# Layer 2 of a conv-attention network: one more piece of experts beside the gathers of a graph, layer norms at the end of an attention head

## The chip, the core and the metric

The kernel runs on one core of a Trainium2 chip. The core has a matrix engine (TensorE, PE in the profile, with weight loads shown apart as PEld), a vector engine (DVE), an activation engine (ACT), GpSimd (POOL) and a queue engine (SP) that issues most of the DMAs. The metric is the device time of one execution in microseconds, and of several executions the median.

## The reference, cut to what matters

A feature map `x` of shape (2, 256, 48, 48) goes through four layers: a selective-scan layer, a convolution-attention layer, and two layers of token mixing and token-wise experts. The change touches layer 2. Its 4608 tokens (2 x 2304, width 256) first go through a split attention, where one third of the positions are queries, one third keys and one third values, and the outputs of three heads stand behind one another; then through a layer norm, a graph attention whose four scores per token choose two of four experts, and the experts:

```python
t = t + _L2_attn_ref(_ln_t(t), ...)      # _ln_t: layer norm over 256 channels
t = t + _L2_ffn_ref(_ln_t(t), ...)

# attention, for each of 3 heads
e = x @ W.T + b;  q, k, v = jnp.split(e, 3, axis=1)      # split along positions
attn = softmax(q @ k.T * SCALE);  out_h = attn @ v

# experts
agg = segment-softmax aggregation of h[src] over all edges (and loops), by dst
scores = layernorm(agg + b_gat).reshape(M, HEADS, NUM_EXPERTS).mean(1)
topk_s, topk_i = top_k(scores, 2);  w = softmax(topk_s)
for ei in range(4):
    g = where(topk_i == ei, w, 0).sum(-1)
    hh = gelu(x @ W1[ei] + b1[ei])
    out = out + g * (hh @ W2[ei] + b2[ei])
```

There are 1,048,576 edges with indices drawn from 0 to 65,535. Indices beyond the 4608 tokens are clipped for the source (so most edges start at the last token), and edges to targets that don't exist are dropped.

## The kernel before, in words

Activations lie with the 256 channels on 128 partitions twice and the 4608 tokens along the free axis, in pieces of 384 columns: 12 pieces, 6 for each of the two batch images. `E.xres` is the running sum, `E.xn` its layer norm.

**Split attention (`layer2_attn`, L700 to L815).** For each image `b` and head `h` PE computes queries (L750), then for six blocks of 128 rows the logits (L764); DVE takes the row maximum, ACT the exponential (L773), DVE the reciprocal and the product (L778), PE transposes the block (L782), and DVE and ACT copy it to `pT`. Behind the blocks stand the sum over the values (L796) and the output projection (L806), added to `E.xres`. While image 1 is worked on, the pieces of image 0 are finished, so their layer norm for the experts is done there: L757 makes two generators per head, and L787 and L788 step one of them after each block. A generator (`normalize_piece`, which uses `layernorm`, L90 to L113) has three steps: DVE adds the two halves (L96); PE takes the mean (L99), DVE subtracts (L100) and ACT squares; PE takes the variance (L107), ACT takes the root, DVE the reciprocal (L110) and the product (L111). The PSUM pool for it has one buffer. The six pieces of image 1 are normalized at the beginning of `layer2_ffn`, in pairs in lock step.

**Experts and graph (`layer2_ffn`, `graph_scores`).** What an expert gives for a token doesn't need the graph; only its weight `g` does. So the pieces of 384 tokens fall into four sorts, set by L1322:
- `pieces(0, AHEAD)`, two pieces, run while the node part of the graph is worked on.
- `pieces(AHEAD, BESIDE)`, four pieces, run beside the gathers. POOL gathers rows of two tables for the last edges of each list (L1050 and L1054, 64 each, `add_edges`); meanwhile `count_last` counts, in 32 groups, how many of the clipped edges go to each target: DVE writes one-hot rows in bf16 (L946, L950), PE sums them (L952, 32 matmuls a group). `behind_gathers` takes the steps of the expert pieces between these groups in proportion, `n_beside` steps over 32 groups; a piece has 24 steps.
- `pieces(BESIDE, EARLY)`, two pieces, behind the graph's last edges (L1080, L1082, L1086), while the scores are worked out on DVE.
- the last `12 - EARLY`, four pieces, `later`, with the weights known.

For the early pieces the four experts' outputs are written to DRAM (`y_d`, L1375) and read back by `join` (L1410), which spreads the weights over the partitions on PE (L1402), multiplies on DVE (L1411) and adds on POOL (L1412). The last loop takes each late piece with `EARLY / n_late` joins, two at a time, and steps the layer norms of finished pieces between its matmuls.

One early piece has 4 experts, each of 8 matmuls with Gelu on ACT (L1354, L1358) and 8 for the second product (L1369) with the bias on ACT (L1373).

The order on each engine is not the program's: a scheduler reorders instructions of a block by its own estimates of durations. In the kernel before, the first four chunks of eight edges in `add_edges` have their L1063 to L1072 between count groups, though they are written behind `beside()`.

Of the kernel before, what the change touches and what calls it, by code (L numbers as in the profile page):

```python
# [33 lines left out]
NCH = L // W  # L34
# [417 lines left out]
def normalize_piece(E, wp, ps, c, eps=1e-5):  # L452

    cs = slice(c * W, (c + 1) * W)
    yield from layernorm(E, wp, ps, E.xres[:, :, cs], E.xn[:, :, cs], eps)
# [230 lines left out]
@with_exitstack  # L686
def layer2_attn(ctx, E):

    nc, tc, p = E.nc, E.tc, E.p
    NH, D = 3, 768
    S = L // NH
    DT, ST, HW2 = D // P, S // P, S // 2
    scale = C**-0.5
    big = ctx.enter_context(tc.tile_pool(name="l2big", bufs=1))
    xn = E.xn
    gm = big.tile([P, NH, 2, 2 * C], F32, name="gm")
    ub = big.tile([P, NH, 4], F32, name="ub")  # L700
    with (
        tc.tile_pool(name="l2wt", bufs=2) as wts,
        tc.tile_pool(name="l2wps", bufs=2, space=PSUM) as ps,
    ):
        for h in range(NH):

            w_eo = wts.tile([P, DT, 2 * C], F32, tag="w_eo", name="w_eo")
            nc.sync.dma_start(w_eo[:, :, 0:C], p["W_embed"][h].rearrange("(k p) m -> p k m", p=P))
            nc.sync.dma_start(w_eo[:, :, C:], p["W_outT"].rearrange("(k p) m -> p k m", p=P))
            for m in range(2):  # L710
                pg = ps.tile([P, 2 * C], F32, tag="pg", name="pg")
                for k in range(DT):
                    nc.tensor.matmul(
                        pg, lhsT=w_eo[:, k, m * P : (m + 1) * P], rhs=w_eo[:, k, :],
                        start=k == 0, stop=k == DT - 1,
                    )
                nc.vector.tensor_copy(gm[:, h, m, :], pg)
            pu = ps.tile([P, 4], F32, tag="pu", name="pu")
            for m in range(4):
                for k in range(DT):  # L720
                    nc.tensor.matmul(
                        pu[:, m : m + 1], lhsT=w_eo[:, k, m * P : (m + 1) * P],
                        rhs=E.v("b_embed", h * DT + k, 1), start=k == 0, stop=k == DT - 1,
                    )
            nc.vector.tensor_copy(ub[:, h, 0:2], pu[:, 0:2])
            nc.vector.tensor_tensor(ub[:, h, 2:4], pu[:, 2:4], E.v("b_out"), ALU.add)

    act = ctx.enter_context(tc.tile_pool(name="l2act", bufs=2))
    wp = ctx.enter_context(tc.tile_pool(name="l2w", bufs=2))
    ps = ctx.enter_context(tc.tile_pool(name="l2ps", bufs=3, space=PSUM))  # L730
    pss = ctx.enter_context(tc.tile_pool(name="l2pss", bufs=2, space=PSUM))
    psn = ctx.enter_context(tc.tile_pool(name="l2psn", bufs=1, space=PSUM))

    for b in range(NB):
        t0 = b * L
        xv = act.tile([P, ST, C], F32, tag="xv", name="xv", bufs=1)
        for t in range(ST):
            o = t0 + 2 * S + t * P
            tp = ps.tile([P, C], F32, tag="mm", name="tp")
            for k in range(2):  # L740
                nc.tensor.transpose(tp[:, k * P : (k + 1) * P], xn[:, k, o : o + P], E.ident)
            nc.vector.tensor_copy(xv[:, t, :], tp)
        for h in range(NH):
            qq = act.tile([P, 2, S], F32, tag="qq", name="qq")
            for m in range(2):
                for g in range(2):
                    gs = slice(g * HW2, (g + 1) * HW2)
                    pq = ps.tile([P, HW2], F32, tag="mm", name="pq")
                    for k in range(2):
                        nc.tensor.matmul(  # L750
                            pq, lhsT=gm[:, h, k, m * P : (m + 1) * P],
                            rhs=xn[:, k, t0 + g * HW2 : t0 + (g + 1) * HW2], start=k == 0, stop=k == 1,
                        )
                    nc.scalar.activation(qq[:, m, gs], pq, AF.Identity, bias=ub[:, h, m : m + 1])


            norms = [normalize_piece(E, wp, psn, (b - 1) * NCH + c) for c in range(2 * h, 2 * h + 2) if b]  # L757
            pT = act.tile([P, ST, S], F32, tag="pT", name="pT", bufs=1)
            for t in range(ST):
                sp = pss.tile([P, 2, 512], F32, tag="sp", name="sp")  # L760
                for g in range(2):
                    o = t0 + S + g * HW2
                    for k in range(2):
                        nc.tensor.matmul(  # L764
                            sp[:, g, :HW2], lhsT=qq[:, k, t * P : (t + 1) * P],
                            rhs=xn[:, k, o : o + HW2], start=k == 0, stop=k == 1,
                        )
                mx = wp.tile([P, 1], F32, tag="mx", name="mx")
                nc.vector.tensor_reduce(mx, sp[:, :, :HW2], AX.XY, ALU.max)
                nc.vector.tensor_scalar(mx, mx, -scale, None, ALU.mult)  # L770
                pr = wp.tile([P, S], F32, tag="pr", name="pr")
                sm = wp.tile([P, 1], F32, tag="sm", name="sm")
                nc.scalar.activation(  # L773
                    pr.rearrange("p (g w) -> p g w", g=2), sp[:, :, :HW2], AF.Exp,
                    bias=mx, scale=scale, accum_out=sm,
                )
                nc.vector.reciprocal(sm, sm)
                nc.vector.tensor_scalar(pr, pr, sm, None, ALU.mult)  # L778
                for n in range(0, ST, 3):
                    tp = ps.tile([P, 3, P], F32, tag="mm", name="tp")  # L780
                    for j in range(3):
                        nc.tensor.transpose(tp[:, j, :], pr[:, (n + j) * P : (n + j + 1) * P], E.ident)  # L782
                    if n:
                        nc.scalar.copy(pT[:, n : n + 3, t * P : (t + 1) * P], tp)
                    else:
                        nc.vector.tensor_copy(pT[:, n : n + 3, t * P : (t + 1) * P], tp)
                if norms:  # L787
                    next(norms[t // 3])  # L788

            ox = act.tile([P, 2, S], F32, tag="ox", name="ox")  # L790
            for m in range(2):
                for g in range(2):
                    gs = slice(g * HW2, (g + 1) * HW2)
                    po = ps.tile([P, HW2], F32, tag="mm", name="po")
                    for n in range(ST):
                        nc.tensor.matmul(  # L796
                            po, lhsT=xv[:, n, m * P : (m + 1) * P], rhs=pT[:, n, gs],
                            start=n == 0, stop=n == ST - 1,
                        )
                    nc.scalar.copy(ox[:, m, gs], po)  # L800
            for m in range(2):
                for g in range(2):
                    o = t0 + h * S + g * HW2
                    py = ps.tile([P, HW2], F32, tag="mm", name="py")
                    for k in range(2):
                        nc.tensor.matmul(  # L806
                            py, lhsT=gm[:, h, k, C + m * P : C + (m + 1) * P],
                            rhs=ox[:, k, g * HW2 : (g + 1) * HW2], start=k == 0, stop=k == 1,
                        )
                    y = wp.tile([P, HW2], F32, tag="y", name="y")  # L810
                    nc.vector.scalar_tensor_tensor(
                        y, py, ub[:, h, 2 + m : 3 + m], xn[:, m, o : o + HW2], ALU.add, ALU.add
                    )
                    xr = E.xres[:, m, o : o + HW2]
                    nc.gpsimd.tensor_tensor(xr, xr, y, ALU.add)  # L815

# [496 lines left out]
def layer2_ffn(ctx, E, edges):  # L1315
# [3 lines left out]

    nc, tc, p = E.nc, E.tc, E.p  # L1320
    NX, FT = 4, 4
    AHEAD, BESIDE, EARLY = 2, 6, 8  # L1322
    big = ctx.enter_context(tc.tile_pool(name="l2fbig", bufs=1))
    xn = E.xn
    w1 = big.tile([P, NX, 2, 512], F32, name="w1")
# [12 lines left out]
    wp = ctx.enter_context(tc.tile_pool(name="l2fw", bufs=2))  # L1338
# [50 lines left out]
    psn = ctx.enter_context(tc.tile_pool(name="l2fpn", bufs=2, space=PSUM))  # L1389
# [50 lines left out]
    for i in range(n_late):  # L1440
# [5 lines left out]
        norms = chain.from_iterable(normalize_piece(E, late, psn, c) for c in done)  # L1446
# [498 lines left out]
```

## Time and profile before

| | us |
|---|---|
| three timed executions | 5452.36, 5459.55, 5462.36 (median 5459.55) |
| the profiled execution | 5504.47, span 5502.7, mean granted TensorE clock 0.949 |
| split attention of layer 2 | 3182 to 3515 |
| first two expert pieces, node part | 3515 to 3640 |
| gathers, count, four pieces | 3640 to 3933 |
| the edges' sums (L1086) | 3933 to 4010 |
| two pieces and the scores | 4010 to 4100 |
| joins and late pieces | 4100 to 4362 |

The stage limits are from the trace; layers 0 and 1 lie ahead of them and layer 3 behind. A row of the timeline gives start and duration in us, the engine, the line, the operation, output and inputs with shape, and how many instructions; in brackets stands how long the engine idled before and what released it. [...]

### The profile page before, as it was taken

The numbers are of one execution on the slowest core, as the hardware profiler recorded it, in microseconds if no ns is written. First come the engines' busy times: TensorE is split into PE (matmuls) and PEld (weight loads), VectorE is DVE, ScalarE is ACT, GpSimd is POOL, SyncE is SP. The second block draws the span as 40 slices with busy tenths as digits, with TensorE's granted clock in tenths as the row PEclk, the third lists the DMA queues.
The fourth block names the chain that finished last, engine by engine and source line by source line (L and its number), as shares of the span: only waits on it lengthen the run. The fifth ranks groups of instructions, "written<-read, shape, count | busy, mean of one in ns | idle before, by whom it ended". The sixth has DMA issues, their size and how long they took to land. (4 is left out here: it accounts for less than half of the span.)

```text
span 5502.7 us, 47222 instructions
## 1 busy us (share of the span) xinstructions
PE 4797.7 (87%) x15246; PEld 2649.9 (48%) x15246; DVE 3499.6 (64%) x5380; ACT 2371.5 (43%) x4935; POOL 2398.4 (44%) x1295
## 2 busy tenths in 40 slices
PE   7888788888877787879999999998799999998996
PEld 3444344444333343435555555565455555554664
DVE  4899988888999888999994234456534401212333
ACT  5767777666767566622222123322023322222220
POOL 3888887888989888830000000048412100001112
PEclk8999999999999899999999899999899999999997
DMA  4444444443444444421100100111111100001323
GB/s 155 166 171 177 165 178 160 160 157 137 173 150 173 150 161 153 151 100 37 41 26 2 39 1 0 37 38 24 14 58 46 46 6 6 9 6 23 83 76 80
DMA packets 173646, 486.56 MB, mean 88 GB/s; under 512 B 31487, under 2 KB 96516, under 8 KB 173124
## 3 DMA queue, kind: packets, MB, share of 16 engines
q1 hardware_dynamic: 165252, 471.82, 24.3%
q0 software_dynamic: 8128, 11.55, 1.6%
q8 instruction: 124, 2.03, 0.1%
q14 instruction: 142, 1.16, 0.1%
HBM read 416.44 MB, written 66.86 MB: 88 GB/s over the span
## 5 line engine op out<-in xcount | busy, mean ns | idle before, releaser
L344 PE MATMUL yp<-hc,ident 128*128 128x384 f32 x3072 | 1199.9, 523 | 293.7 <-DVE hc L390 253.8
L359 POOL TENSOR_TENSOR db<-dtu,bb 128x1536 f32<-128x1536 f32 x384 | 1333.3, 3473 | 45.5 <-issue 16.5
L344 PEld LDWEIGHTS yp<-hc,ident 128*128 128x128 f32 x3072 | 574.7, 198 | 875.3 <-DVE hc L390 451.3
L390 POOL TENSOR_TENSOR hc<-ho,cc 128x384 f32<-128x384 f32 x576 | 582.6, 1020 | 183.6 <-DVE ho L382 81.9
L390 DVE TENSOR_TENSOR hc<-hs,cc 128x384 f32<-128x384 f32 x960 | 501.3, 544 | 38.9 <-PE yp L344 37.7
L376 ACT ACTIVATE hs<-dt,negab 128x384 f32<-128x384 f32 x768 | 435.2, 582 | 92.6 <-DVE ho L385 41.4
L376 ACT ACTIVATE hs<-dt,negaf 128x384 f32<-128x384 f32 x768 | 434.6, 582 | 58.4 <-DVE hc L390 27.7
L385 DVE TENSOR_TENSOR_SCAN hs<-hs,state,db 128x384 f32<-128x384 f32 x400 | 396.6, 1015 | 55.8 <-POOL db L359 30.3
L382 DVE TENSOR_TENSOR_SCAN hs<-hs,state,db 128x384 f32<-128x384 f32 x400 | 397.1, 1014 | 30.0 <-POOL db L359 23.2
L1770 POOL DMA_INDIRECT xe<-xt_d,token x48 | 52.4, 1091 | 726.4 <-issue 715.0
L266 PE MATMUL mm<-xw,w_cv 128*128 128x384 f32 x768 | 288.8, 512 | 64.5 <-ACT xs L270 26.6
L1704 PE MATMUL po<-at,xtok 128*128 128x384 f32 x864 | 329.7, 506 | 7.7 <-ACT at L1702 7.5
L912 POOL PARTITION_ALL_REDUCE most<-most x1 | 0.4, 382 | 738.8 <-DVE most L911 738.8
L1354 PE MATMUL ph<-xn,w 128*128 128x384 f32 x768 | 292.9, 523 | 28.0 <-issue 10.4
L1695 PE MATMUL sp<-qT,xn 128*128 128x384 f32 x864 | 317.2, 486 | 0.0
L1702 ACT ACTIVATE at<-sp 128x384 f32<-128x384 f32 x216 | 104.9, 491 | 472.5 <-PE sp L1695 472.4
L1358 ACT ACTIVATE hid<-ph,vec 128x384 f32<-128x384 f32 x192 | 110.8, 582 | 338.8 <-PE ph L1354 254.5
L627 PE MATMUL pf<-t,wfc 128*128 128x384 f32 x768 | 255.4, 489 | 0.0
L646 PE MATMUL po<-hid,wfc 128*128 128x384 f32 x768 | 253.6, 486 | 0.0
L385 DVE TENSOR_TENSOR_SCAN ho<-hs,state,db 128x384 f32<-128x384 f32 x240 | 241.2, 1005 | 15.3 <-ACT hs L376 15.1
L382 DVE TENSOR_TENSOR_SCAN ho<-hs,state,db 128x384 f32<-128x384 f32 x240 | 240.3, 1001 | 6.3 <-ACT hs L376 6.2
L266 PEld LDWEIGHTS mm<-xw,w_cv 128*128 128x128 f32 x768 | 146.0, 196 | 192.7 <-ACT xs L270 43.2
(434 smaller groups left out, 7962.9 us busy)
## 6 DMA issues: line engine op xcount, KB each, us to landing
bb<-bcd SPq DMA_DIRECT2D x192, 768.0 KB
cc<-bcd SPq DMA_DIRECT2D x192, 768.0 KB
xw<-xi_d SPq DMA_DIRECT2D x24, 774.0 KB
w<-in_m_w SPq DMA_DIRECT2D x16, 1024.0 KB
y_d<-y SPq DMA_DIRECT2D x32, 384.0 KB
ye<-y_d SPq DMA_DIRECT2D x32, 384.0 KB
xi_d<-xz SPq DMA_DIRECT2D x48, 192.0 KB
z_d<-xz SPq DMA_DIRECT2D x48, 192.0 KB
```

What stands on the lines that cost most here:

```text
L266: nc.tensor.matmul(px, lhsT=w_cv[b, s][:, d * 4 + k, :], rhs=xw[:, d, o : o + W], start=k == 0, stop=k == 3,)
L344: nc.tensor.matmul(yp[d], lhsT=E.ident, rhs=hc, start=False, stop=summed[d] == NS)
L359: nc.gpsimd.tensor_tensor(db, bc(dtu[:, d, :], [P, GN, W], 1), bb, ALU.mult)
L376: nc.scalar.activation(hs, dt[:, d, :], AF.Exp, scale=nega[s][:, d * NS + n : d * NS + n + 1])
L382: nc.vector.tensor_tensor_scan(to, hs, db[:, j], init, ALU.mult, ALU.add)
L385: nc.vector.tensor_tensor_scan(to[:, ::-1], hs[:, ::-1], db[:, j, ::-1], init, ALU.mult, ALU.add)
L390: (nc.gpsimd if on_pool else nc.vector).tensor_tensor(hc, to, cc[:, j, :], ALU.mult)
L627: nc.tensor.matmul(pf, lhsT=wfc1[:, k, f * P : (f + 1) * P], rhs=t1[:, k, :], start=k == 0, stop=k == 1,)
L646: nc.tensor.matmul(po[m], lhsT=wfc2[:, f, m * P : (m + 1) * P], rhs=hid[:, i, :], start=f == 0, stop=f == 15,)
L1354: nc.tensor.matmul(ph, lhsT=w1[:, e, k, f * P : (f + 1) * P], rhs=xn[:, k, c * W : (c + 1) * W], start=k == 0, stop=k == 1,)
L1695: nc.tensor.matmul(sp, lhsT=xn[:, k, t0 + i * P : t0 + (i + 1) * P], rhs=qT[:, k, c * W : (c + 1) * W], start=k == 0, stop=k == 1,)
L1704: nc.tensor.matmul(po[m], lhsT=xtok[:, i, m * P : (m + 1) * P], rhs=at, start=i == 0, stop=i == MT - 1,)
```

## The change

The layer norms of image 0 no longer take a step after each block of a head of image 1. The two pieces of a head are normalized together, in lock step, at the head's end. And `EARLY` goes from 8 to 9 and `BESIDE` from 6 to 7: five pieces instead of four beside the gathers (120 steps instead of 96 over the 32 count groups), two behind the graph as before, and three late pieces with three joins each instead of four with two.

```diff
--- before.py
+++ after.py
@@ layer2_attn
-            norms = [normalize_piece(E, wp, psn, (b - 1) * NCH + c) for c in range(2 * h, 2 * h + 2) if b]
             pT = act.tile([P, ST, S], F32, tag="pT", name="pT", bufs=1)
             for t in range(ST):
...
                     else:
                         nc.vector.tensor_copy(pT[:, n : n + 3, t * P : (t + 1) * P], tp)
-                if norms:
-                    next(norms[t // 3])
...
                     xr = E.xres[:, m, o : o + HW2]
                     nc.gpsimd.tensor_tensor(xr, xr, y, ALU.add)
+
+            if b:
+                norms = [normalize_piece(E, wp, psn, (b - 1) * NCH + 2 * h + i) for i in range(2)]
+                for _ in zip(*norms):
+                    pass
@@ layer2_ffn
     NX, FT = 4, 4
-    AHEAD, BESIDE, EARLY = 2, 6, 8
+    AHEAD, BESIDE, EARLY = 2, 7, 9
```

## The prediction

> **What bounds the kernel now.** I read the page's busy shares first, then a table of windows over the stages that the change touches, then the waits of PE and DVE in the gather stage, then the rows themselves. PE is busy for most of the span:
>
> ```profile
> PE 4797.7 (87%) x15246; PEld 2649.9 (48%) x15246; DVE 3499.6 (64%) x5380; ACT 2371.5 (43%) x4935; POOL 2398.4 (44%) x1295
> ```
>
> The windows are split attention (3182 to 3515), gathers with count and four pieces (3640 to 3933), and joins with late pieces (4100 to 4362). Columns: length, then busy time and instructions of PE, PEld, DVE, ACT, POOL, then granted clock, DMA share, GB/s.
>
> ```profile
> 3182.00:3515.00 333.00, 303.94 (x1037) 181.91 (x1037) 132.61 (x255) 102.84 (x181) 23.86 (x24) 0.94 0.01 2
> ...
> 3640.00:3933.00 293.00, 242.06 (x1529) 162.53 (x1528) 173.42 (x105) 61.27 (x102) 235.29 (x128) 0.91 0.12 24
> ...
> 4100.00:4362.00 262.00, 253.65 (x706) 129.41 (x704) 125.20 (x124) 80.64 (x109) 61.60 (x35) 0.92 0.15 44
> ```
>
> The late stage is full on PE (254 of 262 us): whatever PE no longer does there is gained. The gather stage has 51 us of PE idle, so an extra piece may or may not fit in. Where that idle time lies (PE's waits, 3640 to 4000: total, times, longest):
>
> ```profile
> PE po L1369 <- ACT hid L1358: 29.4, 1, 29.4
> PE ph L1354 <- issue: 10.4, 6, 5.7
> PE ph L1354 <- ACT hid L1358: 5.5, 5, 3.5
> ```
>
> and the rows at the one long wait:
>
> ```profile
> 3920.01 0.95 POOL L1054 DMA_INDIRECT gd<-t_dst,didx  x1 [0.30 <-issue]
> 3926.26 0.20 DVE L957 COPY cnt<-cp 128x36 f32<-128x36 f32 x1 [44.22 <-remote]
> 3926.32 0.58 ACT L1358 ACTIVATE hid<-ph,vec 128x384 f32<-128x384 f32 x1 [34.71 <-remote]
> 3926.95 3.57 PE L1369 MATMUL po<-hid,w 128*128 128x384 f32 x5 [29.37 <-ACT hid L1358]
> ```
>
> The count's matmuls had ended at 3892.4, yet DVE's copy of the count and ACT's Gelu, which need nothing but PE's results, start at 3926.3, 5 us after the last gather. So PE's signals came late while POOL gathered without a pause (3883 to 3921). Whether timed executions lose these 29 us too is the main open question: many semaphore records are missing there, and the profiled execution took 5504.47 us, 44.9 us (0.8%) more than the median of 5459.55, which is what would follow if this wait and the smaller "issue" waits were the recorder's. Everything below is a difference, laid on the median. 0.2%, 10.9 us, is about what a measurement of this kernel can tell from no change.
>
> What paces POOL and DVE in that stage:
>
> ```profile
> 3837.07 0.94 POOL L1054 DMA_INDIRECT gd<-t_dst,didx  x1 [0.30 <-issue]
> 3838.32 0.95 POOL L1050 DMA_INDIRECT gs<-t_src,sidx  x1 [0.30 <-issue]
> 3840.82 4.52 POOL L1050 DMA_INDIRECT gs<-t_src,sidx  x1 [0.30 <-issue]
> ```
>
> ```profile
> 3779.84 0.19 DVE L1068 TENSOR_TENSOR e<-gs,gd 128x32 f32<-128x32 f32 x1 [9.86 <-DMA gd<-t_dst,didx]
> 3780.34 4.41 DVE L946 TENSOR_TENSOR ol<-lo,lo_ids 128x4096 bf16<-128x4096 bf16 x1
> 3806.96 0.19 DVE L1068 TENSOR_TENSOR e<-gs,gd 128x32 f32<-128x32 f32 x1 [16.23 <-DMA gd<-t_dst,didx]
> ```
>
> A gather with its gap takes 1.25 us alone and about 4.7 us beside DVE's one-hot L946 (4.42 us): each count group costs POOL some 3.45 us. The scheduler hoists the first four chunks' L1068 between count groups on DVE; each waits there for its chunk's sixteenth gather, with the next L946 queued behind it and PE's next count group behind that.
>
> **The late stage: four late pieces become three, with three joins each for two.** The rounds start on PE (L1395) at 4161.50, 4224.39, 4288.76; the steady period is 64.37 us. A late piece's own 70 matmuls take 45.2 us at 0.645 (two records of a matmul; eight matmuls took 5.16). A third join adds 4 spreads and 3 transposes, 3.1 us, and a further norm, 1.3: at least 4.4. Half the period's remainder, (64.37 - 45.2)/2 = 9.6, is the upper bound. I take 6.4, since joins run partly at the cold clock (L1402 rows of 0.91 for two records). Three rounds of 70.8 against four of 64.4: -45 us, bounds -51 and -36. The added POOL adds (4 x 1.81) and DVE multiplies (4 x 0.95) lie beside PE; at three joins POOL is busy 22 of 71 us. Without that cover the upper bound applies. The added DMAs, four y_d writes and four ye reads on SP's queue, move 3 MB at a DMA share of 0.12 to 0.15 with four ye buffers: nothing, or some 3 us if the first ye of a join is late.
>
> **The gather stage: a fifth piece.** It brings 64 matmuls x 0.645 = 41.3 us of PE; 16 Gelus and 8 bias adds on ACT (0.58 each, 14 us, ACT is 79% idle). PE gets 10 expert matmuls a group for 8, so a group's period is 2.02 + 6.45 = 8.5 us. The order of the built kernels also changes: before, the chunk waits on DVE stand around groups 16, 20 and 23; after, chunks 0 and 1 stand between groups 9 and 10, and chunks 2 and 3 both ahead of group 13. I walk POOL and DVE with the prices above from 3671.7, up to where nothing differs:
> - Chunk 1 needs gather 32. DVE stands idle from about 3704, POOL runs at 1.25 us, gather 32 ends at 3721, L946 number 10 ends at 3727.4; PE has run out of work some 18 us before.
> - L946 11 and 12 follow by 3741.4; by then 38 gathers are done. Chunk 3 needs number 64: 26 more at 1.25 end at 3774.8, L1068 1.4 us later as in the rows, L946 13 from 3776.8; group 13 on PE at 3782 after another 22 to 26 us of idling.
> - The last 20 groups: 20 x 2.02 + 202 x 0.645 = 170.7, to 3952.7; 2.7 us at the cold clock after the stall (8 records of L1354 took 5.49 us for 2.81) and hiccups of about 10 as now (15.55 us per two groups for 14.4): 3965, bounds 3950 and 3975.
> - Gathers 65 to 128 at 4.5 per 9.1 us end near 3908, before the count, so no unbroken run of gathers stands behind it.
>
> Today the stage ends at 3932.6, or at 3902.6 without the long wait. So it costs +33 us if timed runs have the wait, +63 if not; bounds of the walk +48 to +73 for the latter. The add_edges run behind it (77 us, DVE at 70) is unchanged and starts from the count's end either way. I take +63, for the 44.9 us reason above.
>
> A rule against a row: the Trainium skill, "SBUF — State Buffer", section "Who interferes with whom", says that a tensor_tensor with both inputs in SBUF blocks only GpSimd's reads, and infers that descriptor generation, which needs the write port, is not blocked by it. By that rule 128 gathers would take 160 us, no chunk would be waited for, and the extra piece would cost its 41 us, the sum then -8. The rows here disagree: L946 is a tensor_tensor and the gather beside it takes 4.52 us instead of 0.95, so the sum goes by the rows.
>
> **Split attention: norms at a head's end.** The same 12 pieces (b-1) are normalized; ACT, PE and DVE instructions are only moved. A head without norms has a pitch of 49.1 us (L806 at 3234.72 and 3283.83), those with them 54.1, 57.75, 54.5 and 55.4. Part of that is the tail's wait:
>
> ```profile
> 3267.67 0.84 PE L782 MATMUL tp<-ident,pr 128*128 128x128 f32 x6 [2.48 <-DVE pr L778]
> 3319.56 1.51 PE L782 MATMUL tp<-ident,pr 128*128 128x128 f32 x6 [4.25 <-DVE pr L778]
> 3377.04 1.51 PE L782 MATMUL tp<-ident,pr 128*128 128x128 f32 x6 [4.25 <-DVE pr L778]
> ```
>
> L110's 2.54 us reciprocal stands ahead of the last softmax block on DVE. In the order after, two such tails lose it (1.7 us each); a pair of norms moves instead to the next head's start, where Sqrt and Exp swap tables (1.28 us). Bounds -8 (four tails cleared at 1.8, less a little) and +3 (two swaps unhidden); I take -4, two tails. The PSUM pool of one buffer makes the second norm of a pair wait for the first: DVE's L100 and L111, with the next head's L778 queued behind. That is what would eat the gain. The last pair, behind the loop, stays.
>
> **Sum:** -45 + 63 - 4 = +14: 5459.55 + 14 = 5473.5 us. Its own range, with the bounds of each step partly cancelling: 5460 to 5490.
>
> **Rivals.**
> - A, faster: timed runs do have the 29 us wait, and it goes, since the gathers end before the count. -45 + 33 - 4 = -16: 5443.5. It decides as soon as more than 14 us of that wait is real. For it: PE issues single matmuls 1.2 to 1.4 us apart in bursts of gathers, in step with them. Against: the missing records and the slow profiled run.
> - B, much slower: if PE's signals truly stick behind an unbroken run of gathers, the new 26-gather wait may not end with gather 64: L946 13 misses its buffer's release until number 128. 64 x 1.25 = 80 us more: -16 + 80 = +64, 5523. Against: group 11, whose buffer it needs, ends while L946 12 still slows POOL.
> - C, no change: timed gathers are free of recording and take 0.95, not 1.25 (the 0.30 gap "issue"). The 48 gathers of the two waits shorten by 14 us: +14 - 14 = 0, 5459.5.
>
> **How the numbers follow.** Forecast 50%, A 25%, C 13%, B 12%. Of the forecast's 50, 34 are over +10.9 us, 15 within, 1 below; of A's 25, 21 below and 4 within; C 3 below, 6 within, 4 above; B all above. Faster 0.25, same 0.25, slower 0.50. The range 5436 to 5503 takes in A to 7 us below its value and the forecast with 13 us more than its own upper bound; B and a little of A's low end stay out.
>
> **What would show it.** Right: late rounds 70 to 72 us apart; DVE rows L1068 with waits of about 18 and 34 us; add_edges' matmuls starting near 3965; no wait near 29 us at the last gather; the tails' 4.25 us waits down to 2.5 in two heads. Wrong: rounds of 74 or more, chunk waits under 10 us, a DVE wait of 80 us, or a long wait that stays in the profile.

## The result, and the profile after

The changed kernel took 5465.55 us in the median of 20 runs (5456.7 to 5479.59), the kernel before 5457.02 beside it (5449.6 to 5468.12): a ratio of 1.0016, 95% interval 1.0009 to 1.0024, so 8.5 us slower, with an interval of 5 to 13. The forecast was 5473.5, +14.

The profiled executions say the opposite: 5470.04 us after, 5504.47 before. First the busy shares from the page of the changed kernel, then a table of windows over its three stages (columns as in the prediction):

```profile
span 5468.3 us, 47253 instructions
...
PE 4787.9 (88%) x15242; PEld 2647.6 (48%) x15242; DVE 3499.1 (64%) x5378; ACT 2368.7 (43%) x4941; POOL 2390.3 (44%) x1299
```

```profile
3176.00:3499.00 323.00, 298.30 (x1037) 178.60 (x1036) 134.04 (x255) 99.93 (x179) 23.79 (x24) 0.97 0.01 3
3623.00:3934.00 311.00, 274.83 (x1656) 185.35 (x1655) 173.06 (x104) 74.44 (x126) 225.46 (x128) 0.94 0.13 28
4101.00:4325.00 224.00, 216.50 (x574) 106.76 (x571) 123.51 (x121) 71.46 (x93) 67.92 (x39) 0.89 0.21 58
```

The late stage is 38 us shorter (262 to 224) and still full on PE. The gather stage now holds 275 us of PE work instead of 242. From the first gather to the edges' sums it takes 304.1 us (3629.53 to 3933.66) against 285.6 (3646.95 to 3932.58). Lines moved by one behind the attention: L947 is L946 of before, L1069 is L1068, L1396 is L1395.

The 29 us wait at the last gather is gone; PE's waits in the gather stage (total, times, longest) are now those for DVE:

```profile
PE cp L953 <- DVE oh L951: 33.6, 2, 21.2
PE po L1370 <- ACT hid L1359: 2.4, 1, 2.4
```

DVE's chunk waits stand behind them, in rows of the timeline, with PE's first matmul of group 13 below:

```profile
3683.57 0.19 DVE L1069 TENSOR_TENSOR e<-gs,gd 128x32 f32<-128x32 f32 x1 [5.39 <-DMA gd<-t_dst,didx]
3703.64 0.19 DVE L1069 TENSOR_TENSOR e<-gs,gd 128x32 f32<-128x32 f32 x1 [18.52 <-DMA gd<-t_dst,didx]
3734.43 0.19 DVE L1069 TENSOR_TENSOR e<-gs,gd 128x32 f32<-128x32 f32 x1 [11.45 <-DMA gd<-t_dst,didx]
3754.61 0.24 DVE L1069 TENSOR_TENSOR e<-gs,gd 128x32 f32<-128x32 f32 x1 [20.00 <-DMA gd<-t_dst,didx]
...
3760.37 2.19 PE L953 MATMUL cp<-oh,ol 128*128 128x36 bf16 x32 [21.16 <-DVE oh L951]
```

This is the walk of the prediction: 18.5 us for chunk 1, 11.45 + 20.0 for chunks 2 and 3 together, and PE idling 12.5 and 21.2 us behind them. The rounds of the late stage, and the first transpose of layer 3 behind them:

```profile
4101.22 0.49 PE L1396 MATMUL tp<-ident,g 128*4 128x128 f32 x3
...
4175.23 0.49 PE L1396 MATMUL tp<-ident,g 128*4 128x128 f32 x3
...
4245.54 0.49 PE L1396 MATMUL tp<-ident,g 128*4 128x128 f32 x3
...
4325.28 0.66 PE L1678 MATMUL tp<-ident,xn 128*128 128x128 f32 x4 [0.65 <-DVE xres L1436]
```

74.0, 70.3 and 79.7 us. Before, four rounds took 61.6, 62.9, 64.4 and 73.2 us, between these rows:

```profile
4099.92 0.49 PE L1395 MATMUL tp<-ident,g 128*4 128x128 f32 x3
...
4361.99 0.66 PE L1677 MATMUL tp<-ident,xn 128*128 128x128 f32 x4 [0.65 <-DVE xres L1435]
```

In the attention before, four tails waited 4.25 us or more. The prediction shows the first two; the other two are

```profile
3431.41 1.51 PE L782 MATMUL tp<-ident,pr 128*128 128x128 f32 x6 [4.26 <-DVE pr L778]
3487.60 1.51 PE L782 MATMUL tp<-ident,pr 128*128 128x128 f32 x6 [4.60 <-DVE pr L778]
```

After, the four are

```profile
3311.68 1.51 PE L780 MATMUL tp<-ident,pr 128*128 128x128 f32 x6 [1.84 <-DVE pr L776]
3368.97 1.37 PE L780 MATMUL tp<-ident,pr 128*128 128x128 f32 x6 [4.32 <-DVE pr L776]
3421.83 0.84 PE L780 MATMUL tp<-ident,pr 128*128 128x128 f32 x6 [1.79 <-DVE pr L776]
3472.91 0.84 PE L780 MATMUL tp<-ident,pr 128*128 128x128 f32 x6 [2.48 <-DVE pr L776]
```

so three of the four long waits went, 6.9 us together, and the stage from the first transpose (L741) to the last head's projection shrank from 323.0 to 312.6 us.

What is left to explain is why a trace that is 34 us shorter belongs to a kernel that is 8.5 us slower.

### The profile page after: what moved, and what is told of

It reads as the page before. It is cut to its first block, busy times and chain, and to the rows that moved or that the text cites. A ratio compares the mean times of both kernels' runs of the same rounds, so it can differ in the third digit from the quotient of the medians.

```text
span 5468.3 us, 47253 instructions
## 1 busy us (share of the span) xinstructions
PE 4787.9 (88%) x15242; PEld 2647.6 (48%) x15242; DVE 3499.1 (64%) x5378; ACT 2368.7 (43%) x4941; POOL 2390.3 (44%) x1299
## 5 line engine op out<-in xcount | busy, mean ns | idle before, releaser
L392 ACT COPY state<-hs 128x1 f32<-128x1 f32 x800 | 117.4, 155 | 277.3 <-DVE hc L390 275.5
```

## The experiments

Theory 1, as predicted: the 29.4 us wait is made by the recorder, and timed runs of the kernel before don't have it. Theory 2: it is in timed runs too. The chips decided between them in a way that neither had foreseen: **the kernel before takes about 5451 to 5457 us in the timed runs of some chips and 5501 to 5503 in those of others**. Recorded runs go with the timed ones: the kernel with 32 idle gathers more took 5449.55 us recorded beside a median of 5451.76 on a chip of the first kind, 5542.85 beside 5532.98 on one of the second. I call them prompt and late chips. Of the four jobs below, each on another chip, the first ran on a prompt one and the other three on late ones. Each chip was seen in one job only, so it is not shown that the chip, and nothing else in the job, makes the difference.

The comparison of the result ran on a prompt chip, by its 5457 us (which chip is not on record). The page of before that the prediction read is of the late kind. Besides its 5504.47 us and its wait, its list of DMAs lacks the time from issue to landing. So do the pages of all eight late runs, while the changed kernel's first page and those of the four prompt runs have it (before, then the changed kernel):

```profile
bb<-bcd SPq DMA_DIRECT2D x192, 768.0 KB
bb<-bcd SPq DMA_DIRECT2D x192, 768.0 KB, 4.2
```

| run | change against the kernel before | before there, us | ratio, 95% interval |
|---|---|---|---|
| e1_norms_only | attention part alone | 5450.93, prompt | 0.9988 (0.9979 to 0.9997) |
| e2_pieces_only | pieces alone | 5450.93, prompt | 1.0042 (1.0028 to 1.0055) |
| e3_more_gathers | 32 idle gathers more | 5450.93, prompt | 1.0002 (0.9993 to 1.0011) |
| e5_before_held | chunks held behind the count | 5450.93, prompt | 1.0008 (0.9999 to 1.0017) |
| e4_after_held | whole change, chunks held | 5502.20, late | 0.9921 (0.9905 to 0.9937) |
| e6_norms_held | attention part, chunks held | 5502.20, late | 0.9975 (0.9965 to 0.9984) |
| e7_piece_behind | ninth early piece behind the graph | 5502.20, late | 0.9994 (0.9985 to 1.0002) |
| e8_change | the whole change | 5501.04, late | 0.9999 (0.9987 to 1.0011) |
| e9_after_held_again | as e4_after_held | 5501.04, late | 0.9925 (0.9909 to 0.9941) |
| e10_more_gathers_again | as e3_more_gathers | 5501.04, late | 1.0058 (1.0043 to 1.0072) |
| e11_after_held_third | as e4_after_held | 5503.05, late | 0.9907 (0.9892 to 0.9922) |
| e12_norms_only_again | as e1_norms_only | 5503.05, late | 0.9978 (0.9968 to 0.9988) |

### Is the wait at the last gather real?

The edit, in `add_edges` of the kernel before:

```diff
     if beside is not None:
+        idle = ip.tile([P, 32, F], F32, name="idle")
+        for j in range(32):
+            nc.gpsimd.indirect_dma_start(
+                out=idle[:, j, :], out_offset=None, in_=t_src[:, :],
+                in_offset=bass.IndirectOffsetOnAxis(ap=sidx[:, j : j + 1], axis=0),
+            )
         beside()
```

> The kernel before, with 32 further gathers behind the 128 real ones, whose rows nobody reads; the order on PE, DVE and ACT is the same. They lengthen POOL's unbroken run behind the count by 32 x 1.25 = 40 us, to about 3961. Theory 1 (the 29.4 us wait of PE and DVE at the end of the run exists only while a profile is recorded): the profiled execution shows the wait grown to about 69 us, and the timed runs stay at those of before within 3 us, ratio 1.000. Theory 2 (the wait is there in timed runs too): both grow, timed runs by about 40 us, ratio 1.007.

The time stayed (1.0002). But the recorded execution did not do what theory 1 says: POOL gathers until 3955, and no long wait stands behind the count. DVE's copy of the count comes at once, and PE's waits from 3640 to the end of the edges' sums are 5.8 us at most (rows of the timeline):

```profile
3864.26 0.20 DVE L957 COPY cnt<-cp 128x36 f32<-128x36 f32 x1 [9.39 <-PE cp L952]
...
3954.35 0.94 POOL L1062 DMA_INDIRECT idle<-t_src,sidx  x1 [0.30 <-issue]
...
3960.05 7.07 PE L1360 MATMUL ph<-xn,w 128*128 128x384 f32 x12 [9.79 <-issue]
```

The 9.8 us in the last row stand behind the edges' sums. SP, ACT, DVE and PE all go on there within 0.7 us (3959.35 to 3960.05), some 4 to 5 us after the last idle gather. At the same place PE stands 5.5 us in the run of the attention part alone, on this chip and without idle gathers. So the idle gathers may cost some 4 us there, but not the 40 that theory 2 expects, and the recorder doesn't make the wait at the count. The same kernel was run on a late chip:

> The kernel before with 32 further gathers. If this is a chip on which the kernel before takes about 5502 us, and PE's signals there wait for POOL's unbroken run to end, the wait grows with the run: +40 us, ratio 1.007, in timed and profiled runs alike. If the wait there is of a fixed length, or if the chip is of the other kind: within 3 us, ratio 1.000.

There it costs 0.58%, 32 us, in timed runs (the expected 1.007 lies in the interval), and the wait has grown to 56.9 us (rows of the timeline):

```profile
3937.41 0.20 DVE L957 COPY cnt<-cp 128x36 f32<-128x36 f32 x1 [60.79 <-remote]
3948.61 0.58 ACT L1364 ACTIVATE hid<-ph,vec 128x384 f32<-128x384 f32 x1 [62.52 <-remote]
3949.25 6.07 PE L1375 MATMUL po<-hid,w 128*128 128x384 f32 x10 [56.90 <-issue]
...
3954.84 0.94 POOL L1062 DMA_INDIRECT idle<-t_src,sidx  x1 [0.30 <-issue]
```

On a late chip, then, DVE and ACT do go on late after PE's results while POOL gathers without a pause, and a longer run makes a longer wait. It grew by 27 us for 40 us of gathers; PE went on 6.5 us before the last one ended, so it isn't simply released by the end. The profile calls the releaser "remote"; whether the signal is sent late or taken late is not in the records.

One kernel, the attention part alone, was recorded on both kinds of chip. On the prompt one DVE's copy of the count waits for PE as in the row above, on the late one PE stands 33.3 us at the last gather (row of the first, then PE's wait in the second):

```profile
3863.55 0.20 DVE L958 COPY cnt<-cp 128x36 f32<-128x36 f32 x1 [9.39 <-PE cp L953]
```

```profile
PE po L1370 <- ACT hid L1359: 33.3, 1, 33.3
```

Why chips differ is open: no run looks at that.

### The two parts apart

The attention part alone is the change without its new `AHEAD, BESIDE, EARLY`:

> The attention part of the change alone (norms at a head's end; pieces as before). Theory: the two traces show the split attention 10.4 us shorter (PE's L741 to the last head's projection, 323.0 against 312.6), of which about 1.7 lies in a head without norms and is the granted clock; so the part by itself is worth 8 to 9 us: ratio near 0.9985, 5449 us against 5457. Rival: the shorter stage is the clock of one profiled execution, and the timed runs show nothing: ratio 1.000, within 2 us.

> The attention part alone. Theory: worth the same on either kind of chip, since its stage has no gathers: ratio 0.998 to 0.999. Rival (a gain of that size is the difference of two chips or clocks): 1.000.

It gains 0.12% on the prompt chip and 0.22% on a late one: 6.5 and 12 us, intervals 2 to 11 and 7 to 18. The stage is 312.3 and 312.6 us in these two traces, and 321.1 to 323.0 wherever the old order ran (the runs with 32 idle gathers, with the pieces alone, with four pieces held, and the kernel before). The rival (the difference of two chips or clocks, ratio 1.000) lies outside both intervals; the sizes agree with the 9 to 10 us of the traces within them.

The pieces alone are the kernel before with this one line changed:

```diff
-    AHEAD, BESIDE, EARLY = 2, 6, 8
+    AHEAD, BESIDE, EARLY = 2, 7, 9
```

> The fifth piece beside the gathers alone (norms as before). Theory: it costs what the whole change costs plus what the norms gain: 8.5 + 8.5 = +17 us, ratio 1.003. In its profile the gather stage lasts as long as after the change (304 us from first gather to the edges' sums), the late stage 224 instead of 262, and no PE wait of 20 us or more stands at the last gather. Rival (norms worth nothing): +8.5 us, ratio 1.0016.

1.0042 is +23 us (15 to 30). Two other traces of this job have the pieces as before: the run with idle gathers and the attention part alone. Against them the stretch from the first gather to the first join takes 470.3 us instead of 412.4 and 409.7, +58 and +61; the late stage takes 228.4 instead of 262.3 and 268.3, -34 and -40. The sums are +24 and +21. No PE wait of 20 us stands at the last gather, but two for DVE stand ahead of groups 10 and 13, as after the whole change. The expected +17 lies in the interval, the rival's +8.5 outside it.

### The same change on a late chip

> The changed kernel itself beside the kernel before on one chip. So far the chips are of two kinds: on one the kernel before takes 5451 us and no wait follows the last gather, on the other 5502 us with a wait of about 30 us in its profiled and its timed runs. Theory (the wait belongs to the chip, not to the recorder): where the kernel before takes about 5451 to 5457 us, the change costs 8 to 14 us (ratio 1.0016 to 1.0025); where it takes about 5502, the change gains some 34 us, as between the two profiled executions (ratio 0.994). Rival (the wait is a recording's): ratio 1.0016 on either.

Neither: 0.9999, within 7 us of no change. The gain of 34 us that I took from the two profiled executions compares two kinds of chip. On this late chip the stretch from the first gather to the edges' sums takes 339.2 us, 53.6 more than the 285.6 of before. The wait at the last gather is gone, as the gathers end at 3864 and the count goes on, but another stands in the middle (timeline; DVE's wait for chunk 3, PE's wait, and a later wait of DVE):

```profile
3748.61 0.19 DVE L1069 TENSOR_TENSOR e<-gs,gd 128x32 f32<-128x32 f32 x1 [19.73 <-DMA gd<-t_dst,didx]
...
3763.44 2.93 PE L1355 MATMUL ph<-xn,w 128*128 128x384 f32 x4 [26.43 <-ACT hid L1359]
...
3808.78 4.42 DVE L947 TENSOR_TENSOR ol<-lo,lo_ids 128x4096 bf16<-128x4096 bf16 x1 [15.93 <-remote]
```

While DVE waits for chunks 2 and 3, POOL gathers without a pause; PE, which needs a Gelu from ACT, stands 26.4 us, and twice 8 us later on. In the first trace of the changed kernel, on a prompt chip, POOL has the same run of 26 gathers there (32 us), and PE waits only for the one-hot behind the chunk. So by these traces the wait moved from the end of the run of gathers to the runs that the chunk waits make.

### Without the chunk waits

The edit makes DVE's first use of a chunk depend on the count, so no chunk can stand between two count groups:

```diff
-def add_edges(E, pools, keys, t_src, t_dst, lo_row, hi_row, fp, beside=None):
+def add_edges(E, pools, keys, t_src, t_dst, lo_row, hi_row, fp, beside=None, hold=None):
...
         rows = cp.tile([P, GQ, F], F32, tag="rows", name="rows", bufs=2)
+        if hold is not None and q < 2:
+            nc.vector.tensor_copy(e, hold[:, : GQ * H].rearrange("p (i h) -> p i h", h=H))
         nc.vector.tensor_tensor(e, gs[:, :, 0:H], gd[:, :, 0:H], ALU.add)
...
-            add_edges(E, (ip, cp), edges.oth, t_src, t_dst, lo_row, hi_row, fp, behind_gathers)
+            add_edges(E, (ip, cp), edges.oth, t_src, t_dst, lo_row, hi_row, fp, behind_gathers, edges.cnt)
```

> The kernel before, with the chunks' L1068 held behind the count (a copy of the count into the first two e tiles ahead of them, 0.1 us each), so that no count group queues behind a wait for gathers. Theory (a chunk's wait on DVE stalls the count and so PE, 9.9 and 16.2 us of DVE waiting in the trace of before): PE no longer idles for it, the edges' sums start 10 to 15 us sooner in timed runs, ratio 0.9975. Rival (the waits of before are covered by the expert matmuls on PE, and only lost early work remains): 0 to +4 us, ratio 1.000 to 1.0007.

With four pieces on the prompt chip it gains nothing (1.0008), as the rival said. The waits of DVE move behind the count: 18.7 us for chunks whose gathers end at 3920, and PE waits 14.4 us in the edges' sums for DVE (totals of the waits in 3600 to 3990). So with only four pieces beside them the edges' sums still wait for POOL's gathers.

> The changed kernel, with the chunks' L1069 held behind the count as in the run on the kernel before. Theory (the fifth piece costs more than its 41 us because four chunks wait on DVE ahead of count groups 10 and 13, PE idling 12.5 and 21.2 us there): both waits go, the gathers still end before the count does, the stage shortens by 20 to 30 us: about 5440 us, ratio to before 0.997. Rival (POOL's 128 gathers set the end of the stage anyway, so PE's idle time only moves to its end): within 5 us of the changed kernel, ratio 1.0007 to 1.0016.

> The changed kernel with the chunks held behind the count, on the same chip as the changed kernel. Theory (the two waits of DVE ahead of count groups 10 and 13 are part of the fifth piece's price on any chip): 10 to 20 us below the changed kernel. Rival (only its place beside the gathers counts): within 4 us of it.

With five pieces on late chips it is the fastest kernel measured there: 0.9921, 0.9925 and (end of this section) 0.9907, some 41 to 51 us below before, and in the second job 45.6 us below the changed kernel on the same chip (5457.28 against 5502.86). I had expected 10 to 20. PE's largest waits in the stage, in the second job:

```profile
PE ph L1357 <- issue: 7.9, 5, 3.6
PE ph L1357 <- DMA r_ln_beta<-in_g_ln_beta: 5.5, 1, 5.5
```

None is above 5.5 us. DVE's one-hots now go on until shortly before the gathers are done, so the longest run of short gathers (about 1 us each, one behind another) is 10 (12 us, in the first and third of these jobs), where the chunk waits made one of 26 (32 us). The stretch to the edges' sums is 286.8 us, 52.4 less than with the chunk waits. Of this, 35.1 us is what the changed kernel takes longer here than in its first trace (339.2 against 304.1). The other 17.3 would be the price of the chunk waits themselves; this split rests on traces from two kinds of chip and was not tested.

> Norms at a head's end, pieces as before, chunks held behind the count. If the gains of the two add: 8 + 13 = 21 us below before, about 5436, ratio 0.996. If holding is worth nothing with four pieces: that of the norms alone, 0.9985.

With four pieces it does not add on a late chip either: 0.9975 beside 0.9978 for the attention part alone. The count ends sooner, the run of gathers behind it is longer, and the wait at its end is 44.6 us, where the attention part alone has 33.3.

> The changed kernel with the chunks held behind the count, for a chip on which the kernel before takes about 5455 us. Theory (holding takes the 34 us of PE's idle time ahead of groups 10 and 13 away on any chip): 10 to 20 us below the changed kernel, so 0 to 12 us below before, ratio 0.998 to 1.000. Rival (where PE's signals are prompt, four held chunks lose as much early work as they save): ratio 1.0016 like the changed kernel. On a chip of the other kind once more 0.992.

This job's chip was late again (0.9907), so what holding is worth to the changed kernel on a prompt chip was not measured.

### The piece behind the graph

> The kernel before, with the ninth early piece put behind the graph instead of beside the gathers (three pieces there). Theory: behind the graph PE is full, so the piece costs 41.3 us there, and the late stage gains its 38: +3 us, ratio 1.0006, 14 us better than the fifth piece beside the gathers. Rival (a piece beside the gathers is not dearer than its matmuls): the same as that one within 3 us.

`AHEAD, BESIDE, EARLY = 2, 6, 9`: 0.9994, not resolved from no change, where I expected 1.0006, which lies outside the interval. In its trace the stretch from the edges' sums to the joins takes 209.0 us instead of 167.3, +41.7, and the late stage 228.1, -34. The first term is as expected (41.3), the second a little less (38). Their sum is +8, the timed difference -8 to +1; this gap is not explained. The comparison with the piece beside the gathers was meant for one kind of chip and is not made by this run, as no run of the pieces alone stands beside it.

## Why the prediction was right, and where not

**Late stage, -45 with bounds -51 and -36:** -38 between the two pages, -34 and -40 in the runs of one job. The steady round was right (70.3 us for 70.8). The first one was not: it took 74.0 where its predecessor took 61.6, +12.4 for a third join that I had priced at 6.4, and rounds of 74 or more were my own sign of being wrong. The stage was mis-sized by 5 to 11 us, outside the near bound in one comparison. The row that I named for the cold clock was misread, too: two records of L1402 in 0.91 us are no slower than two of L1354 (0.91 at 4226.94); the slow ones take 1.64 (4242.50).

**Gather stage, +63 with bounds +48 and +73:** +64 to the edges' sums and +58 to +61 to the joins, on the prompt chip. The mechanism is the forecast one: 41 us of matmuls, and chunk waits of 18.5 and 31.5 us on DVE (forecast 18 and 34) with PE idling 12.5 and 21.2 us (forecast 18 and 22 to 26). The edges' sums started 304 us after the first gather instead of the 318 of the walk; on a prompt chip before has 238 instead of the 256 that I took for it. Both walks held hiccups of about 10 us, and the steady count of before shows none on the prompt chip: two groups took 14.5 us in the run with idle gathers, against the 15.5 of the page that I read. The two errors, 14 and 17 us, nearly cancelled in the difference.

**That the 29 us wait was the recorder's: wrong in its reason.** It is on the chip, in timed runs too. The page that I read is of the late kind, the three times beside it of the prompt kind. All three hints that I took for the recorder, the 44.9 us between page and median, the "issue" waits among the count groups and the missing records, go with the late chips. Leaving the wait out of the timed difference was right only because the runs that were compared are from a prompt chip, and that was luck: on a late one the change measured 0.9999.

**Attention, -4 with bounds -8 and +3:** -9 to -10 in the traces, -6.5 and -12 in timed runs. Three tails cleared, where I counted on two, and by 2.1 to 2.5 us each instead of 1.7; PE's waits for the softmax product fell from 24.0 to 16.5 us in the stage. The heads with norms went from 54.1, 57.75, 54.5 and 55.4 us to 51.6, 57.6, 51.2 and 51.1. The swaps of tables and the wait for the one PSUM buffer, which I let eat part of the gain, cost less than that.

**The rule against the row:** the trace of after agrees with the rows of before. The 128 gathers took 264 us from the first start to the last end (3629.53 to 3893.69). The rule of the Trainium skill, "SBUF — State Buffer", section "Who interferes with whom", would have given 160 for a tensor_tensor.

**The sum** by measured terms, the first two from the run of the pieces alone, is +21 to +24 less 9 to 10: +11 to +15, beside the measured 8.5 with its interval of 5 to 13. The errors of the first and third term, +5 to +11 and -5 to -6, partly cancelled.

**Rivals.** A (the wait is real and goes) named what happens on late chips, but the gain doesn't appear there either: the gather stage lengthens by 53.6 us instead of A's 33. B's mechanism (signals stuck behind the run that chunk 3 needs) fits what takes A's gain there, at about 21 us (53.6 less 33), not 80. The run of gathers did not go on to number 128. C (timed gathers are faster than recorded ones) needs recorded runs that are some 14 us longer than timed ones. With the five pieces beside the gathers they were 4.5 us (the changed kernel, 5470.04 beside 5465.55) and 2.4 us longer (the pieces alone, 5481.46 beside 5479.09).

## What to carry to other kernels

Before a wait is called the recorder's, lengthen what it waits for and look at timed runs; and compare a page only with times from the same chip. Filling one engine's idle time with another piece of work is worth only what the schedule leaves idle afterwards. Here the instruction that a scheduler moved forward on DVE, between two groups that fed PE, made a wait: on late chips the change gained nothing with it and 41 to 51 us without it. On a prompt chip PE idled 33.6 us for it, and holding it back was not measured with the five pieces. Such an instruction is found in the row behind the wait, and held back with a dependency.

## What the runs showed of the hardware

- The same kernel takes 5451 us on one chip and 5501 to 5503 on three others. The mean granted clock in these timed runs is 0.951 on the one and 0.948 on the others, but the clock is not where the time goes: in the two traces of the attention part alone the stretch from the first gather to the edges' sums takes 238.1 us on the prompt chip and 282.9 on a late one, 44.8 us more, while the recorded runs differ by 39.5 in all (5452.43 and 5491.97).
- On the late chips ACT and DVE take up PE's results late while POOL issues gathers without a pause. PE's wait was 29.4, 31.1, 33.3 and 44.6 us behind runs of 38.5, 39.7, 42.2 and 52.3 us, so it grows with the run, and 56.9 with 32 idle gathers more. In the changed kernel ACT stood 33.9 us over a run of 32 us on a late chip, and over the same run on a prompt chip no engine's wait of 5 us or more has "remote" as its releaser.
- A gather beside a bf16 tensor_tensor of DVE (L946, 4.4 us) takes 3.7 to 5.6 us instead of 0.95, mostly 4.2 to 4.9, on either kind of chip.
